# Splitting the node tiles into four chunks instead of three, and letting more expert steps into the rounds of a fused graph kernel

## The chip, the cores and the metric

The kernel runs on one core of one Trainium2 chip. The metric is device time in microseconds (us) of one execution. Engine names are those of the profile: PE is TensorE (PEld its weight loads), DVE is VectorE, ACT is ScalarE, POOL is GpSimd, SP is SyncE, which here only issues DMAs.

## The reference, cut to what matters

6,250 nodes of 256 features and 100,000 edges sorted by destination pass through four layers, each added to its input. All of it is float32.

```python
x = x + gat(layernorm(x), edges)              # attention, 8 heads: softmax over the edges of a node
x = x + moe32(layernorm(x))                   # top-1 of 32 experts: relu(relu(x W1[e] + b1) W2[e] + b2)
x = x + rgcn(layernorm(x), W[16], edges)      # out[dst] += norm * (x[src] @ W[rel])
x = x + moe8(layernorm(x), gamma, beta)       # 2 of 8 experts for the whole batch, then a layer norm
```

The change touches the second layer and the first half of the third: routing of each node to one of 32 experts, the two small matrix products of the expert, and the 16 products `x @ W[rel]` of each node, whose results are a table (`T_tab`) that the third layer gathers from edge by edge.

## The kernel before, in words

**Groups and rounds.** The edges are cut into 98 groups of 1,024. A first loop runs over `g` from 0 to 100; one pass is called a round here. For group `g`, POOL gathers 8 x 128 rows of `H_tab` by edge source (line L468, `hs`, five buffers); DVE scales them by the attention term (`gat_scale`, L603); PE sums them into a window of 128 nodes (`quarters`, L526, then `place`, L542); DVE adds the window into a ring of node tiles (`add`, L550). The parts of one group lie in successive rounds: round `g` adds group `g-3`, places group `g-2`, sums group `g-1` and gathers group `g`. So the two L550 additions of group `g-3` mark the start of round `g`, and round `r` lasts from the addition of group `r-3` to that of group `r-2`.

**Flow.** Beside the attention the same loop carries the next layer, in four kinds of step, each a Python generator (class `Flow`): kind 0, `take` (T), reads four finished node tiles out of the ring and normalizes them; kind 1, `route` (R), computes expert choices and slots, and at its end scatters all rows of the chunk into `x_sort`, sorted by expert (L902, POOL, one scatter per tile); kind 2, `experts` (E), walks over the sorted rows; kind 3, `products` (P), gathers the expert results back (L991, `yg`, POOL), normalizes and multiplies with the 16 relation matrices (L1037, two 512-column outputs per tile and relation pair, one P step each), writing `T_tab`.

**Chunks.** The 49 node tiles are cut into `CHUNKS`. A chunk's experts can begin only when its last row has been scattered, and its products only when its last expert step has been done. Every expert's rows are padded to a multiple of 128, so a chunk of `nt` tiles has up to `nt + 31` sorted tiles (`xt`). `experts` takes them in pairs: it loads 512 KB of sorted rows (L964, `xs`), two expert weight sets (L958, `w`, 192.5 KB each), transposes (L951), multiplies (L940, L928), adds on DVE (L930, `ys`, three buffers) and writes 256 KB (L974, `y_sort`). It is a pipeline of five further steps, so a chunk with `p` pairs takes `p + 5` E steps. All chunks share one `x_sort`; `route` of a chunk waits until the chunk before has read it (`ck.free`).

**Who decides the order.** The loop is recorded under a manual schedule for PE, DVE, ACT and SP: instructions stand on these engines in the order in which the Python code issues them. Once in every round, between the addition and the placement, `fill` draws steps. It has a budget of PE and of DVE microseconds, and each step returns its nominal cost (an E step 3.0 and 0.8, a P step 1.9 and 0.2). The kinds are tried in the order T, R, E, P, with a limit of each per round, as long as PE's budget lasts; all but P also need DVE's budget:

```python
if limits[kind] and left[0] > 0 and (kind == 3 or left[1] > 0):
```

When the 98 groups are over, the rest is drawn by `fill(2.5, 8.0, (1, 1, 1, 1))` until nothing is left. This is called the drain here. In it an E step spends the whole budget, so products wait until the experts of the last chunk are through. After the drain the third layer gathers from `T_tab` in a second loop of 98 groups (L468, `ts`), beside the fourth layer.

Of the kernel before, what the change touches and what calls it, by code (L numbers as in the profile page):

```python
# [47 lines left out]
def gnn_ffn_kernel(  # L48
# [31 lines left out]
    NT = (N + P - 1) // P  # L80
# [4 lines left out]

    RING = 8

    CHUNKS = [(0, 6), (6, 22), (22, NT)]


    blocks = [(t, min(4, NT - 1 - t), P) for t in range(0, NT - 1, 4)]
# [92 lines left out]

    largest = max(CHUNKS, key=lambda c: min(N, c[1] * P) - c[0] * P)
    chunks = [Chunk(*largest)]
    chunks = [chunks[0] if c == largest else Chunk(*c, x_sort=chunks[0].x_sort) for c in CHUNKS]
    whole = Chunk(0, NT)

    class Clear:  # L190
# [5 lines left out]
        def step(self, n):  # L196
            for c in range(self.done, min(self.done + n, self.n)):
                nc.sync.dma_start(self.rows[c], zeros[:, None, :].to_broadcast([P, 2 * D // P, P]))
            self.done = min(self.done + n, self.n)
# [352 lines left out]
    def gat_rows(gr):  # L552

        return gr.gather(H_tab[:, :], gr.idx0, HW, "hs", 1 if gr.dynamic else 5)

    def gat_dest(gr):

        oT = gr.onehot_t()
        if not gr.dynamic:
            return oT, gr.aw  # L560
        b = gr.block()
        aw = gr.pool.tile([P, 2 * HEADS], F32, name="aw")
        nc.vector.tensor_scalar(aw, adsh[:, ds(b, 1), :].rearrange("p o c -> p (o c)"), gr.win(0), None, op0=ALU.mult)
        nc.vector.scalar_tensor_tensor(aw, adsh[:, ds(b + 1, 1), :].rearrange("p o c -> p (o c)"), gr.win(1), aw,
                                       op0=ALU.mult, op1=ALU.add)
        return oT, aw

    def gat_pick(gr, parts, psum):

        oT, aw = parts  # L570
        pq = psum.tile([P, 512], F32, name="pe")
        ex = pq[:, T * 2 * HEADS : T * 3 * HEADS].rearrange("p (t h) -> p t h", t=T)
        if gr.dynamic:
            pe = pq[:, : T * 2 * HEADS].rearrange("p (t h) -> p t h", t=T)
            for t in range(T):
                nc.tensor.matmul(pe[:, t, :], lhsT=oT[:, t, :], rhs=aw, start=True, stop=True)
            return pe, ex

        w = Q * 2 * HEADS
        for u in range(QT):  # L580
            nc.tensor.matmul(pq[:, u * w : (u + 1) * w], lhsT=oT[:, u, :], rhs=aw.rearrange("p q h -> p (q h)"),  # L581
                             start=True, stop=True)
        return pq[:, : QT * w].rearrange("p (u q h) -> p q u h", u=QT, q=Q), ex

    def gat_terms(gr, hs, dest):

        pe, ex = dest

        z = gr.pool.tile([P, T, 2 * HEADS], F32, name="z")
        split = (lambda a: a) if gr.dynamic else (lambda a: a.rearrange("p (q u) h -> p q u h", u=QT))  # L590
        nc.vector.tensor_tensor(split(z), split(hs[:, :, D:]), pe, ALU.add)
        dz = gr.pool.tile([P, T, HEADS], F32, name="dz")
        nc.vector.tensor_tensor(dz, z[:, :, :HEADS], z[:, :, HEADS:], ALU.max)
        if gr.dynamic or gr.g == NG - 1:

            nc.vector.tensor_scalar_min(dz, dz, 0.0)
        nc.scalar.activation(ex, dz, AF.Exp)
        nc.scalar.copy(hs[:, :, D:HA], ex)  # L598

    def gat_scale(hs, dest):  # L600
        hv = hs[:, :, :D].rearrange("p t (h d) -> p t h d", h=HEADS)
        pv = dest[1].rearrange("p t (h o) -> p t h o", o=1)
        nc.vector.tensor_tensor(hv, hv, pv.to_broadcast([P, T, HEADS, HD]), ALU.mult)  # L603
# [484 lines left out]
    with ExitStack() as es_flow:  # L1088
        flow = Flow(es_flow, 2, 3)
        es = ExitStack()  # L1090
        pg = es.enter_context(tc.tile_pool(name="ge", bufs=2))
        pr1 = es.enter_context(tc.tile_pool(name="ge1", bufs=1))
        pp = es.enter_context(tc.tile_pool(name="ge_p", bufs=2, space=PSUM))
        pi = es.enter_context(tc.tile_pool(name="ge_i", bufs=1, space=PSUM))
        aws = [pr1.tile([P, Q, 2 * HEADS], F32, name=f"aw{i}") for i in range(6)]
        for a in aws:
            nc.vector.memset(a, 0.0)
        ring = Ring(pr1.tile([P, RING + 1, HA], F32, name="ring"))
        nc.vector.memset(ring.t, 0.0)

        done = [-1]

        def ready(tiles):

            return done[0] >= min(NG - 1, tiles * P * NG // N + 1)

        flow.after = lambda ck: tails.append(flow.products(ck))
        for before_ck, ck in zip([None] + chunks, chunks):
            ck.free = lambda c=before_ck: c is None or c.sorted
        takes = [flow.take(ck, ring, ready) for ck in chunks]  # L1110
        for ck in chunks:
            ck.taken = []
        routes = [flow.route(ck) for ck in chunks]
        runs, tails = [], []

        def step(kind):

            q = (takes, routes, runs, tails)[kind]
            while q:
                c = next(q[0], -1)  # L1120
                if c == -1:
                    q.pop(0)
                    if kind == 1:
                        runs.append(flow.experts(chunks[len(chunks) - len(q) - 1]))
                    continue
                return c
            return None

        left = [0.0, 0.0]

        def fill(pe, dve, limits):

            left[:] = min(left[0], 0) + pe, min(left[1], 0) + dve
            limits, any_ = list(limits), False
            while left[0] > 0:
                some = False
                for kind in range(4):
                    if limits[kind] and left[0] > 0 and (kind == 3 or left[1] > 0):
                        limits[kind] -= 1
                        c = step(kind)  # L1140
                        if c is None:
                            limits[kind] = 0
                            continue
                        some = any_ = True
                        left[:] = left[0] - c[0], left[1] - c[1]
                if not some:
                    break
            return any_


        with tc.manual_schedule(engines={PE, DVE, ACT, SP}):

            boot = flow.consts(cleared)
            groups = [Group(pg, g, False) for g in range(NG)]
            for g in range(4):
                if g < 3:
                    groups[g].load_dst()
                groups[g].load_terms(aws[g])
            dest = {0: gat_pick(groups[0], gat_dest(groups[0]), pp)}
            rows, hots, aggs, sums = {}, {}, {}, {}  # L1160
            for g in range(NG + 3):
                if g < NG:
                    rows[g] = gat_rows(groups[g])
                if g >= 3:
                    drained.append(ring.drained)
                    groups[g - 3].add(sums.pop(g - 3), HA, ring.t, True)
                    done[0] = g - 3
                if 2 <= g < NG + 2:
                    parts = groups[g - 2].leave(aggs.pop(g - 2), HA)
                if g < NG:  # L1170
                    hots[g] = groups[g].onehot(False)
                if g + 1 < NG:
                    oT = gat_dest(groups[g + 1])
                if g + 3 < NG:
                    groups[g + 3].load_dst()
                if g + 4 < NG:
                    groups[g + 4].load_terms(aws[(g + 4) % 6])
                next(boot, None)
                fill(6.5, 5.0, (3, 3, 3, 9))
                if 2 <= g < NG + 2:  # L1180
                    sums[g - 2] = groups[g - 2].place(pi, parts, HA)
                if g + 1 < NG:
                    dest[g + 1] = gat_pick(groups[g + 1], oT, pp)
                if 0 < g <= NG:
                    gat_scale(rows[g - 1], dest[g - 1])
                    aggs[g - 1] = groups[g - 1].quarters(pi, hots.pop(g - 1), rows.pop(g - 1), HA)
                if g < NG:
                    gat_terms(groups[g], rows[g], dest[g])
        es.close()
        with tc.manual_schedule(engines={PE, DVE, ACT, SP}):  # L1190
            while takes or routes or runs or tails:
                fill(2.5, 8.0, (1, 1, 1, 1))
# [598 lines left out]
```

## Time and profile before

| | us |
|---|---|
| median of 15 runs (3081.93 to 3092.66) | 3088.08 |
| the profiled execution's own time | 3084.9 |
| its span in the profile | 3083.1 |
| start to the first gather of the first loop | 112.4 |
| rounds 0 to 20, before the first expert step | 112.4 to 369.3 |
| rounds 21 to 99 | 369.3 to 1300.7 |
| round 100 and the drain, to the last product | 1300.7 to 1925 |
| second loop and fourth layer | 1925 to 3083.1 |

The times of rounds are read from the start of the L550 additions. Busy shares of the span are PE 73%, PEld 37%, DVE 38%, ACT 28% and POOL 54%, and the 16 DMA engines move 179 GB/s on average. These are averages over stages with different limits, so they are read stage by stage.

### The profile page before, as it was taken

The numbers are of one execution on the slowest core, as the hardware profiler recorded it, in microseconds if no ns is written. First come the engines' busy times: TensorE is split into PE (matmuls) and PEld (weight loads), VectorE is DVE, ScalarE is ACT, GpSimd is POOL, SyncE is SP. The second block draws the span as 40 slices with busy tenths as digits, with TensorE's granted clock in tenths as the row PEclk, the third lists the DMA queues.
The fourth block names the chain that finished last, engine by engine and source line by source line (L and its number), as shares of the span: only waits on it lengthen the run. The fifth ranks groups of instructions, "written<-read, shape, count | busy, mean of one in ns | idle before, by whom it ended". The sixth has DMA issues, their size and how long they took to land. (4 is left out here: it accounts for less than half of the span.)

```text
span 3083.1 us, 32452 instructions
## 1 busy us (share of the span) xinstructions
PE 2245.8 (73%) x8909; PEld 1153.3 (37%) x8910; DVE 1168.5 (38%) x3013; ACT 871.2 (28%) x1797; POOL 1661.6 (54%) x1712
## 2 busy tenths in 40 slices
PE   5534366688476688938999999566766666999984
PEld 4312144344344344416444444112322222555551
DVE  7444535557245555621100000123322222433457
ACT  2212223344233344413343343001111111222253
POOL 0477655777756777330000000777777777777724
PEclk9755566588666788978999999556766666999998
DMA  9567688577887577569544444633433333443424
GB/s 284 144 165 189 206 275 263 162 218 224 275 254 243 162 233 221 186 239 342 216 169 171 168 169 150 194 105 119 125 104 111 111 111 112 139 121 117 123 95 131
DMA packets 372122, 550.82 MB, mean 179 GB/s; under 512 B 88726, under 2 KB 234964, under 8 KB 371920
## 3 DMA queue, kind: packets, MB, share of 16 engines
q1 hardware_dynamic: 263964, 296.00, 28.5%
q0 software_dynamic: 82096, 231.26, 26.3%
q10 hardware_dynamic: 25860, 21.28, 2.3%
q8 instruction: 77, 1.26, 0.2%
q14 instruction: 125, 1.02, 0.1%
HBM read 355.59 MB, written 199.06 MB: 180 GB/s over the span
## 5 line engine op out<-in xcount | busy, mean ns | idle before, releaser
L468 POOL DMA_INDIRECT hs<-H_tab,src_i x784 | 760.9, 970 | 453.0 <-issue 210.5
L468 POOL DMA_INDIRECT ts<-T_tab,idx1b x784 | 755.8, 964 | 331.3 <-issue 233.1
L1037 PE MATMUL pb<-wr,xTt 128*128 128x512 f32 (+1 forms) x1568 | 710.1, 609 | 5.1 <-ACT xTt L1014 3.9
L526 PE MATMUL qagg<-ts,oh 128*32 128x256 f32 x1568 | 314.8, 509 | 192.5 <-DMA ts<-T_tab,idx1b 190.7
L1037 PEld LDWEIGHTS pb<-wr,xTt 128*128 128x128 f32 (+1 forms) x1568 | 299.7, 195 | 371.3 <-issue 356.4
L1040 ACT COPY tr<-pb 128x512 f32<-128x512 f32 (+1 forms) x392 | 228.3, 585 | 427.3 <-PE pb L1037 353.4
L533 ACT COPY qs<-qagg 128x264 f32<-128x264 f32 (+1 forms) x196 | 73.6, 376 | 881.6 <-PE qagg L526 858.5
L991 POOL DMA_INDIRECT yg<-y_sort,slot x49 | 47.1, 961 | 444.3 <-ACT xl L749 281.4
L581 PE MATMUL pe<-aw,oT 128*128 128x64 f32 x392 | 88.1, 368 | 265.9 <-DVE hs L603 90.5
L478 DVE TENSOR_TENSOR oh<-iota,rlm 128x256 f32<-128x256 f32 x196 | 83.3, 425 | 450.7 <-PE qagg L526 450.4
L526 PEld LDWEIGHTS qagg<-ts,oh 128*32 128x32 f32 x1568 | 66.1, 124 | 420.7 <-DMA ts<-T_tab,idx1b 352.6
L603 DVE TENSOR_TENSOR hs<-hs,pe 128x2048 f32<-128x2048 f32 x98 | 223.2, 2278 | 0.6 <-ACT hs L598 0.6
L542 PE MATMUL agg<-qs,pl 128*128 128x264 f32 (+1 forms) x392 | 177.4, 545 | 59.0 <-ACT qs L533 38.6
L1472 PE MATMUL pb<-xT,w 128*128 128x512 f32 (+2 forms) x416 | 196.0, 623 | 0.2 <-ACT xT L1442 0.2
L581 PEld LDWEIGHTS pe<-aw,oT 128*128 128x128 f32 x392 | 78.5, 273 | 311.3 <-issue 194.3
L1481 PE MATMUL pb<-w,h 128*128 128x256 f32 x784 | 175.4, 381 | 2.5 <-ACT h L1474 2.4
L346 DVE RECIPROCAL rst<-sdt 128x2 f32<-128x2 f32 (+1 forms) x25 | 4.1, 165 | 416.9 <-ACT sdt L344 416.9
L526 PE MATMUL qagg<-hs,oh 128*32 128x264 f32 x1568 | 159.3, 544 | 0.0
L1481 PEld LDWEIGHTS pb<-w,h 128*128 128x128 f32 x784 | 147.1, 190 | 28.7 <-issue 5.4
L550 DVE SCALAR_TENSOR_TENSOR ring<-agg,win,ring 128x264 f32 x196 | 96.6, 493 | 136.3 <-PE agg L542 102.9
L550 DVE SCALAR_TENSOR_TENSOR acc<-agg,win,acc 128x256 f32 x196 | 94.7, 483 | 136.3 <-PE agg L542 116.6
L542 PEld LDWEIGHTS agg<-qs,pl 128*128 128x128 f32 x392 | 86.5, 254 | 155.8 <-ACT qs L533 103.8
(297 smaller groups left out, 2461.0 us busy)
## 6 DMA issues: line engine op xcount, KB each, us to landing
T_tab<-tr SPq DMA_DIRECT2D x384, 256.0 KB
xs<-x_sort SPq DMA_DIRECT2D x70, 512.0 KB
w<-w_tab SPq DMA_DIRECT2D x142, 192.5 KB
y_sort<-ys SPq DMA_DIRECT2D x70, 256.0 KB
x_sort<-zeros SPq DMA_DIRECT2D x58, 256.0 KB
db<-in_dst_dram ACTq DMA_DIRECT2D x392, 32.0 KB
hs<-H_tab,src_i POOLq DMA_INDIRECT x784
ts<-T_tab,idx1b POOLq DMA_INDIRECT x784
```

The source lines that it names most:

```text
L468: nc.gpsimd.indirect_dma_start(out=hs[:, t, :], out_offset=None, in_=table, in_offset=bass.IndirectOffsetOnAxis(ap=idx(t), axis=0))
L478: nc.vector.tensor_tensor(oh, iota[:, None, :n].to_broadcast([P, T, n]), column(self.rl), ALU.is_equal)
L526: nc.tensor.matmul(ps[q * QW : (q + 1) * QW, :width], lhsT=oh[:, t, :], rhs=vals[:, t, :width], start=u == 0, stop=u == QT - 1)
L533: nc.scalar.copy(qs, ps[:, :width])
L542: nc.tensor.matmul(ps[:, :width], lhsT=pl, rhs=qs, start=True, stop=True)
L550: nc.vector.scalar_tensor_tensor(a, ps[:, :width], self.win(w), a, op0=ALU.mult, op1=ALU.add)
L581: nc.tensor.matmul(pq[:, u * w : (u + 1) * w], lhsT=oT[:, u, :], rhs=aw.rearrange("p q h -> p (q h)"), start=True, stop=True)
L603: nc.vector.tensor_tensor(hv, hv, pv.to_broadcast([P, T, HEADS, HD]), ALU.mult)
L1037: nc.tensor.matmul(pr[:r, :], lhsT=xT[:, k, j * P : j * P + r], rhs=self.wr[:, k, q0 : q0 + 2, :], start=k == 0, stop=k == KC - 1)
L1040: nc.scalar.copy(o2, pr[:r, :])
L1472: nc.tensor.matmul(ph[:, :nn], lhsT=s.w1[:, k, c * P : (c + 1) * P], rhs=xT[:, k, :nn], start=k == 0, stop=k == KC - 1)
L1481: nc.tensor.matmul(po[:, q * D : (q + 1) * D], lhsT=hid[c][:, (j + q) * P : (j + q + 1) * P], rhs=s.w2[:, c, :], start=c == 0, stop=c == N ...
```

## The change

`CHUNKS` gets four chunks, of 6, 12, 16 and 15 tiles, instead of 6, 16 and 27. In `fill`, E steps are no longer held back when DVE's budget is spent. In the rounds of the first loop, the limit of E steps goes from three to four, and PE's budget is 11.0 instead of 6.5 while no chunk is in its products (`tails` is empty).

```diff
-    CHUNKS = [(0, 6), (6, 22), (22, NT)]
+    CHUNKS = [(0, 6), (6, 18), (18, 34), (34, NT)]
...
-                    if limits[kind] and left[0] > 0 and (kind == 3 or left[1] > 0):
+                    if limits[kind] and left[0] > 0 and (kind > 1 or left[1] > 0):
...
-                fill(6.5, 5.0, (3, 3, 3, 9))
+
+                fill(6.5 if tails else 11.0, 5.0, (3, 3, 4, 9))
```

The numbers of pairs follow from the tile counts: 19, 24 and 29 in the three chunks before, 19, 22, 24 and 23 in the four after.

## The prediction

> **What bounds the kernel now.** I read the table of 40 slices first, then busy times by stretch. The stretches begin and end at L550 additions, so they are whole rounds: 21 to 34 (chunk 1's experts), 35 to 54, 55 and 56, 57 to 71 (chunk 2's experts), 72 to 99 (chunk 2's products); then the drain's routing, its scatters, chunk 3's experts, and products. The columns are length, busy time of PE, PEld, DVE, ACT and POOL, PE's granted clock, DMA share, GB/s.
>
> ```profile
> 369.30:556.90 187.60, 125.60 (x652) 81.72 (x651) 87.28 (x176) 55.87 (x142) 111.64 (x116) 0.65 0.80 249
> 556.90:768.00 211.10, 164.32 (x724) 83.81 (x727) 128.39 (x300) 92.07 (x195) 159.76 (x164) 0.81 0.70 206
> 768.00:811.60 43.60, 12.03 (x62) 7.75 (x63) 11.02 (x29) 4.56 (x13) 32.63 (x34) 0.50 0.78 264
> 811.60:1012.60 201.00, 143.53 (x761) 96.76 (x761) 102.01 (x201) 64.25 (x163) 120.31 (x123) 0.69 0.81 250
> 1012.60:1300.70 288.10, 237.97 (x1032) 119.49 (x1032) 157.29 (x336) 129.40 (x271) 197.14 (x203) 0.87 0.69 204
> 1300.70:1343.00 42.30, 29.44 (x94) 14.89 (x92) 25.97 (x106) 15.01 (x30) 0.02 (x1) 0.92 0.41 145
> 1343.00:1395.00 52.00, 7.17 (x15) 2.83 (x15) 0.27 (x2) 1.76 (x3) 26.53 (x27) 0.57 0.78 284
> 1395.00:1487.00 92.00, 81.90 (x467) 61.20 (x468) 20.04 (x30) 34.64 (x87) 0.00 (x0) 0.91 1.02 363
> 1487.00:1925.00 438.00, 435.22 (x1053) 194.32 (x1051) 21.63 (x124) 169.71 (x307) 26.20 (x27) 1.00 0.45 165
> ```
>
> Three regimes are to be seen. Rounds with products (rows 2 and 5) take 211.1/20 = 10.56 and 288.1/28 = 10.29 us, 10.4 together, a few idle ones included; POOL's gathers follow each other there at about 10 us per group. Rounds with experts take 201.0/15 = 13.4 us (row 4) at a DMA share of 0.81, with POOL busy only 60%: something other than gathers holds them. The drain's experts have the DMA engines saturated (1.02, 363 GB/s): 92 us for 29 pairs, 3.17 us a pair. The drain's products have PE saturated (435 of 438 us): 249 P steps, 1.76 us each.
>
> What holds an expert round is next, in the timeline of round 64, which draws three E steps.
>
> ```profile
> 909.88 1.02 DVE L550 SCALAR_TENSOR_TENSOR ring<-agg,win,ring 128x264 f32 x2 [0.34 <-PE agg L542]
> ...
> 925.66 0.69 DVE L930 SCALAR_TENSOR_TENSOR ys<-pb,xs 128x512 f32<-128x512 f32 x1 [9.51 <-DMA y_sort<-ys]
> ...
> 929.35 1.02 DVE L550 SCALAR_TENSOR_TENSOR ring<-agg,win,ring 128x264 f32 x2 [0.34 <-issue]
> ```
>
> From addition to addition it takes 19.5 us, and 9.51 of them DVE stands before `ys`, whose buffer is still being written to `y_sort`; everything behind it on DVE, `gat_scale` first, stands too. Expert rounds are bound by transfers, through an in-order engine. The last view is the waits from 768 to 825 us, where chunk 2's experts begin.
>
> ```profile
> PE pt L951 <- DMA xs<-x_sort: 25.2, 2, 23.8
> DVE ring L550 <- PE agg L542: 21.9, 1, 21.9
> ```
>
> PE waits for the first sorted rows, which wait for the last of 16 scatters, and the ring addition waits behind it. Rounds 55 and 56 took 43.6 us; at 13.4 each they would have taken 27, so a chunk of 16 tiles pays 17 us to begin.
>
> **The change part by part.** The instruction order of the built program, counted round by round, gives what moves. Rounds 0 to 20 draw the same T and R steps. Then:
> - before: 24 E steps in rounds 21 to 34, 29 in 55 to 71, products in the others, 34 E and 261 P in the drain;
> - after: 24 E in 21 to 27, products from 30 to 46, 27 E in 47 to 54, products from 58 on, 29 E mixed with one P a round in 80 to 100, 28 E and 255 P in the drain.
>
> So the smaller last chunk does not shorten the drain's products: only 6 P steps leave it, because chunk 3's 128 wait there instead. The loop gains 27 E steps: 21 new ones (16 pairs more by padding, 5 pipeline steps of one more chunk) and 6 from the drain.
>
> *The drain.* Its experts fall from 29 to 23 pairs, at 3.17 us: -19 us. Its scatters fall from 27 to 15, but the queue of POOL now has chunk 3's first six `yg` gathers ahead of and between them. 27 scatters took 41.5 us (1343.0 to 1384.5), 1.54 each; the new 21 POOL operations take between 21 x 1.28 = 27 and 32, and the third gather pair waits for a `yg` buffer, 0 to 8 more: -14 to -2, I take -10. Routing has 12 tiles fewer in its slot sums: four blocks instead of seven, each three DVE operations of 0.29 us, -2.6. After the last expert step there are 248 P steps instead of 249: -1.8. Sum: -33 us, bounds -37 and -25. The P steps of the routing part (12 before, 7 after) lie beside R steps; were that cover gone, 5 x 1.76 = 9 us would go as well.
>
> *Rounds 21 to 99 before: 931.4 us.* After, by kind of round:
> - 44 rounds with products or no steps (28 to 46, 55 to 79) at 10.4: 458 us. Density of T, R and P is as before.
> - 15 burst rounds (21 to 27, 47 to 54) with 3.4 E steps and 2.73 pairs each. Upper bound: the three-step round, 19.5, so 20. Lower bound by transfers: row 4 had 0.81 x 201 = 163 us of DMA time; its 22.5 pairs account for 71, leaving 6.1 per round; 6.1 + 2.73 x 3.17 = 14.8. By the chain of engines: an empty round takes 5.9 (two between 1012.6 and 1024.4), an E step 3.2 (from one L928 group to the next, 942.1 to 945.4), so 5.9 + 3.4 x 3.2 = 16.8. I take 18, nearer the three-step row: 270 us.
> - 20 mixed rounds (80 to 99) with 1.35 E and one P. Upper bound 13.4, as row 4 with 1.73 E. Lower bound 10.6, by transfers (6.1 + 1.2 x 3.17, and a P writes 0.26 MB) and by the gathers alike. E steps by row 4's price, (201 - 15 x 5.9)/26 = 4.33 with T and R in it, make 5.9 + 5.8 = 11.7; a P costs nothing if it fills a wait and 1.76 if not. I take 12.3: 246 us.
> - Waits for scatters: three chunks begin in this part instead of two. 17 us for chunk 3, somewhat less for 12 tiles, little for the first: 35, bounds 20 and 55.
>
> The sum is 1009, so +78 us; all lower bounds give 912, all upper bounds 1081.
>
> *The conditions in `fill`.* That E steps no longer need DVE's budget costs nothing itself: L930 is 0.69 us on a DVE that is busy 102 of 201 us. It is what makes the bursts. What stands behind each such L930 is `gat_scale`, and POOL waits for that through the five `hs` buffers. Eleven tiles fewer of `x_sort` to clear (256 KB each) free at most 11 x 0.256 MB / 250 GB/s = 11 us of transfers around rounds 19 to 30; I take that as part of the burst's range.
>
> *Second loop and fourth layer:* the same instructions in the same order, 1158 us, from a later start.
>
> Sum: +78 - 33 = +45 us on the profiled execution of 3084.9, so 3130. The median of the runs is 3.2 above that execution; on it the forecast is 3088 + 45 = **3133 us**.
>
> The loop's 22 additional pairs are 25.4 MB, 101 us at row 4's 250 GB/s and 70 at the 363 that experts reach without gathers; the bounds of the burst rounds lie as far apart. A rule that speaks against the change is in the Trainium skill, "DMA: Bandwidth & Descriptors", section "Issuing engines are not separate DMA queues": transfers started by any engine run on the same 16 DMA engines and interleave, so by it the gathers on POOL's queue give the experts on SP's queue no transfer time of their own. The page's "Where 436 GB/s comes from" puts the HBM limit of a core near 358 GB/s, by which, as an estimate, the 25.4 MB would take 71 us; the trace's 363 lies slightly above.
>
> In favour speaks row 4's clock, 0.69, against 0.91 where the drain's experts run back to back: denser bursts could run at the latter, where an E step takes 2.65 us (1413.00 to 1415.65): 15 x 3.4 x 0.55 = 28 us less, if the chain of engines held the bursts. By the 9.5 us before `ys` it doesn't, so I take nothing for it.
>
> **The rivals.** *A, bursts saturate the transfers, faster.* Mechanism: with four E steps in line DVE always has one whose buffer is free, so bursts run at the DMA floor of 14.8 us and mixed rounds at 10.6 to 11.5. Then the loop is 458 + 222 + 212 to 230 + 30 = 922 to 940, and the change -42 to -24: 3046 to 3064. For it: the drain does reach 1.02. Against: no round with gathers beside experts does; the three-step round shows a 9.5 us stall, not an overlap. It decides at 15 us per burst round with mixed rounds at 12.3, or 16.5 with mixed rounds at 11.2.
>
> *B, bursts starve the loop.* With `aw`, `xs`, `w` and `y_sort` on one SP queue, every wait for a buffer delays the next round's terms, so four-step rounds take 20 or more and each chunk pays its 17 us in full: +150 - 33 = +117, 3205. For it: `ACT pe L597 <- DMA aw<-ad_tab` is among the waits of row 4's stretch (15.3 us). Against: only the two E phases suffer.
>
> *C, the change does little.* Were the new E steps to fill POOL's idle 40% in expert rounds, loop and drain would balance: within 6 us of 3088. The drain's products being nearly as many is for it, the DMA share of 0.8 against.
>
> **How the numbers follow.** Forecast (+10 to +90 us): 0.60; A: 0.20; B (over +90): 0.13; C: 0.07. The range reaches into A and B until 0.15 is left out, 3052 to 3198; the forecast's own is 3098 to 3178. Faster by over 0.2% (about what a measurement of this kernel can tell from no change): 0.20; within: 0.07; slower: 0.73.
>
> **What would show it.** In the profile after, round 28 should begin near 500 us (before 472), round 47 near 698 (694), round 55 near 857 (768), round 80 near 1117 (1102), round 100 near 1378 (1301). The drain from there to the last product should take 592 us, not 624. Burst rounds should show L930 waiting for `y_sort` at a DMA share near 0.9. A is right if burst rounds come at 15 us. The forecast is wrong if round 100 begins before 1344.

## The result

The changed kernel takes 3125.21 us (median of 6 runs, 3118.6 to 3126.34; the profiled run and one more took 3124.94 and 3130.65) against 3087.24 for the kernel before (31 runs): a ratio of 1.0119, with an interval of 1.0108 to 1.0131. It is slower by 38 us; the forecast was slower by 45. The profiled execution has a span of 3123.2 us, against 3083.1.

The first view is again the busy time by stretch, cut at L550 additions, with the columns explained above: rounds 21 to 27, 28 to 46, 47 to 54, 55 to 78, 79 alone, 80 to 99; then the drain's routing, its scatters, chunk 4's experts and the products. Kernel after:

```profile
371.70:501.40 129.70, 95.79 (x470) 65.50 (x469) 46.10 (x89) 38.32 (x98) 60.28 (x64) 0.67 0.81 265
501.40:704.60 203.20, 159.63 (x706) 81.95 (x709) 124.27 (x294) 93.36 (x194) 148.89 (x152) 0.81 0.70 205
704.60:868.40 163.80, 105.19 (x532) 72.32 (x524) 58.24 (x110) 43.22 (x110) 77.49 (x81) 0.68 0.79 260
868.40:1130.00 261.60, 211.97 (x914) 108.45 (x914) 151.73 (x358) 118.04 (x247) 196.95 (x204) 0.84 0.73 219
1130.00:1161.20 31.20, 6.79 (x39) 3.76 (x37) 5.52 (x15) 6.68 (x15) 22.79 (x24) 0.67 0.82 276
1161.20:1377.20 216.00, 172.79 (x957) 107.30 (x957) 121.32 (x243) 81.77 (x203) 121.69 (x126) 0.83 0.84 263
1377.20:1418.00 40.80, 25.54 (x74) 12.86 (x72) 23.26 (x92) 10.48 (x21) 3.77 (x4) 0.78 0.37 129
1418.00:1460.00 42.00, 2.90 (x11) 1.89 (x11) 1.53 (x7) 1.97 (x4) 17.03 (x17) 0.50 0.67 235
1460.00:1530.00 70.00, 63.75 (x365) 47.59 (x363) 16.30 (x25) 27.45 (x69) 0.00 (x0) 0.92 1.00 358
1530.00:1970.00 440.00, 433.02 (x1050) 193.38 (x1050) 21.78 (x125) 169.84 (x307) 24.31 (x25) 1.00 0.46 165
```

Read it by the same regimes. Rounds with products (rows 2 and 4) run as before, 10.69 and 10.90 us each. Bursts (rows 1 and 3) run at 18 us a round, round 47's wait aside, with PE at two thirds of its clock and the DMA engines at 0.8, no fuller than the expert rounds of before. The mixed rounds (row 6) take 10.8 us each, and at a share of 0.84 they are the fullest rounds with gathers in either kernel. The drain's experts last 70 us between these cuts, and 73.5 from their first transpose (1456.1), which is where the 92 of before begin; the share is saturated in both. The products take 440 instead of 438.

| stage (us) | before | after | change |
|---|---|---|---|
| up to round 21 | 369.3 | 371.7 | +2.4 |
| rounds 21 to 99 | 931.4 | 1005.5 | +74.1 |
| round 100 to the first `ts` gather | 632.2 | 596.7 | -35.5 |
| from there to the end of the span | 1150.2 | 1149.3 | -0.9 |

How a burst runs is seen in the timeline of round 49, which draws four E steps. It is the counterpart of round 64 above; the brackets give the idle time before, and what ended it.

```profile
763.63 1.02 DVE L550 SCALAR_TENSOR_TENSOR ring<-agg,win,ring 128x264 f32 x2 [0.48 <-PE agg L542]
...
779.25 0.69 DVE L930 SCALAR_TENSOR_TENSOR ys<-pb,xs 128x512 f32<-128x512 f32 x1 [8.44 <-DMA y_sort<-ys]
...
783.35 0.69 DVE L930 SCALAR_TENSOR_TENSOR ys<-pb,xs 128x512 f32<-128x512 f32 x1 [3.40 <-DMA w<-w_tab]
...
787.02 1.02 DVE L550 SCALAR_TENSOR_TENSOR ring<-agg,win,ring 128x264 f32 x2 [0.33 <-PE pe L581]
```

It lasts 23.4 us, and for 8.44 of them DVE stands before the third `ys`, whose buffer is still being written out, as it did for 9.51 before. Before the fourth, the profile puts 3.40 us down to the weights, a transfer again.

Each chunk still pays to begin. Two waits of round 47, where chunk 2's experts start:

```profile
PE pt L951 <- DMA xs<-x_sort: 31.6, 1, 31.6
DVE ring L550 <- PE agg L542: 29.7, 1, 29.7
```

PE stands before the first sorted rows and the ring addition behind it. Round 47 lasts 39.7 us where the other seven of its burst average 17.7, so the start costs 22. Chunk 3's start falls into round 79, 31.2 us against 10.9 for the rounds before it, so 20.

### The profile page after: what moved, and what is told of

It is laid out like the page before. It is cut to its first block, busy times and chain, and to the rows that moved or that the text cites. A ratio compares the mean times of both kernels' runs of the same rounds, so it can differ in the third digit from the quotient of the medians.

```text
span 3123.2 us, 33300 instructions
## 1 busy us (share of the span) xinstructions
PE 2283.8 (73%) x9163; PEld 1185.1 (38%) x9164; DVE 1183.8 (38%) x3068; ACT 894.9 (29%) x1851; POOL 1660.8 (53%) x1712
## 5 line engine op out<-in xcount | busy, mean ns | idle before, releaser
L1037 PE MATMUL pb<-wr,xTt 128*128 128x512 f32 (+1 forms) x1568 | 725.3, 618 | 6.1 <-ACT xTt L1014 6.0
L542 PE MATMUL agg<-qs,pl 128*128 128x264 f32 (+1 forms) x392 | 168.7, 521 | 55.9 <-ACT qs L533 36.5
L930 DVE SCALAR_TENSOR_TENSOR ys<-pb,xs 128x512 f32<-128x512 f32 (+1 forms) x88 | 60.0, 682 | 267.7 <-PE pb L928 127.8
L951 PE MATMUL pt<-ident,xs 128*128 128x128 f32 x346 | 70.8, 338 | 110.4 <-DMA xs<-x_sort 109.6
L526 PE MATMUL qagg<-hs,oh 128*32 128x264 f32 x1568 | 149.6, 515 | 1.6 <-DVE hs L603 1.1
L550 DVE SCALAR_TENSOR_TENSOR ring<-agg,win,ring 128x264 f32 x196 | 96.6, 493 | 134.9 <-PE agg L542 103.5
```

The costliest lines, as they stand in the source:

```text
L526: nc.tensor.matmul(ps[q * QW : (q + 1) * QW, :width], lhsT=oh[:, t, :], rhs=vals[:, t, :width], start=u == 0, stop=u == QT - 1)
L542: nc.tensor.matmul(ps[:, :width], lhsT=pl, rhs=qs, start=True, stop=True)
L550: nc.vector.scalar_tensor_tensor(a, ps[:, :width], self.win(w), a, op0=ALU.mult, op1=ALU.add)
L1037: nc.tensor.matmul(pr[:r, :], lhsT=xT[:, k, j * P : j * P + r], rhs=self.wr[:, k, q0 : q0 + 2, :], start=k == 0, stop=k == KC - 1)
```

## The experiments

The later runs, e1 to e11, were made on three other chips (e1 to e4 on one, e5 to e8 on the next, e9 to e11 on the third), where the kernel before takes 3490 to 3520 us. Ratios below are against it on the same chip, and stages are compared within a chip except where the text says otherwise. Why these chips are slower is a question of its own (last section).

**The two halves apart.** One run has only the new chunks, the other only the new rules of `fill`.

```diff
 # e1: the kernel before with
-    CHUNKS = [(0, 6), (6, 22), (22, NT)]
+    CHUNKS = [(0, 6), (6, 18), (18, 34), (34, NT)]
 # e2: the kernel after with
-    CHUNKS = [(0, 6), (6, 18), (18, 34), (34, NT)]
+    CHUNKS = [(0, 6), (6, 22), (22, NT)]
```

> The four chunks with the old fill (PE budget 6.5, at most three E steps, E steps need DVE's budget). Counted in the instruction order: rounds 21 to 34 as before, chunk 2's and chunk 3's E steps mixed with about one P a round (rounds 46 to 67 and 79 to 99), 32 E and 289 P steps in the drain, 285 of the P steps after the last expert step (before 249, changed kernel 248). Theory 'starts and padding' (the two edits cost separately and add): rounds 21 to 99 take 188 + 33 rounds of products at 10.7 + 42 mixed rounds at 10.8 + two starts of 20 = 935 us against 931 before; the drain gains 33 us as in the changed kernel and loses 36 x 1.76 = 63, so about +30 us on before, 3117. Rival 'the bursts are the whole loss, a fourth chunk is free': within 10 us of before, 3088 to 3098. Rival 'the fourth chunk alone costs all': 3125 or more.

> Three chunks as before with the new fill. Counted in the order: E steps in bursts, rounds 21 to 27 and 55 to 62, 28 P steps more in the loop and 28 fewer after the drain's experts. Theory (edits add): rounds 21 to 99 take 130 + 170 for the bursts as the changed kernel showed and 64 x 10.7 = 685 for the others, 985 against 931, +54; the drain -28 x 1.76 = -49: together +5 us, 3092. Rival 'bursts are the whole loss': 35 to 40 us slower than before, 3125. Rival 'bursts free rounds for products': the burst rounds cost nothing over the spread ones and the 28 products come for nothing, 40 us faster than before, 3045.

Measured: the chunks alone (e1) 3513.89 us, ratio 1.0070 (1.0046 to 1.0095); `fill` alone (e2) 3490.5, ratio 0.9984 (0.9964 to 1.0004). The product is 1.0054, and the whole change, run again later (e6), gave 1.0050 (1.0024 to 1.0075). So the chunks carry the loss. The rules of `fill` are not told from no change here, and whether they give some of the loss back can't be told either, as the intervals of 1.0070 and 1.0050 overlap.

The stages show why. For before, the loop is taken from e3 (below), which has the same instructions in rounds 21 to 99 and ran on the same chip, and the drain from e5, on another of these chips. A P step is one 512-column output, eight for each tile.

| us | before | chunks only | `fill` only |
|---|---|---|---|
| start of round 21 | 426.5 (e3) | 435.2 | 427.4 |
| rounds 21 to 99 | 1105.5 (e3) | 1086.5 | 1148.7 |
| round 100 to first `ts` | 633.3 (e5) | 663.0 | 590.7 |
| P steps after the last E step | 249 | 285 | 221 |

With the old budget the new chunks' E steps push products out of the loop: round 100 begins 10 us earlier (1521.7 against 1532.0) although the loop holds 23 more E steps, and 36 P steps, 63 us at 1.76, reappear in the drain, of which the smaller last chunk saves only about 33. That makes +19, near the +21 of the medians. Of the 19 us by which rounds 21 to 99 are shorter, 9 stand before round 21 instead, because the first chunk's scatters come a round earlier (last section). The expectation had +4 for these rounds and +30 for the drain. With the old chunks the new rules move 28 P steps into the loop: +43 us there, -43 in the drain, as near to nothing as expected (+5). The whole change does both, and ends with the products of the drain where they were (248), so the drain keeps its 33 and the loop bears the E steps. What looked like one trade, experts out of the drain for a longer loop, is two trades of which one cancels.

**The two kernels again.** Both were run unchanged on one later chip, as a reference for the others.

> The kernel before, once more, for its stages on the chip of the runs beside it. The runs before this one fell on a chip on which the kernel before takes 3492 us, so stages are compared with a run of the same chip. All theories: where the chip is as in the first profiles, round 100 starts at 1301 and the span is 3083; on the other, 3490.

> The changed kernel once more, beside the kernel before on the same chip. Theory: 1.2% slower where the kernel before takes 3087 us. Where it takes 3492 us, waits for transfers are longer in all rounds, so the additional expert pairs weigh less against the same bases: 0 to 1.2% slower. By adding the two edits as measured there (chunks alone 1.0070, fill alone 0.9984): 1.0054.

Measured: before (e5) 3512.9 us in one run, against a median of 3520.14 on that chip; after (e6) 3535.72, ratio 1.0050. Rounds 21 to 99 took 1114.3 and 1163.7, +49 where the first chip had +74; the drain 633.3 and 597.6, -35.7 where it had -35.5. So the drain's saving is the same to a microsecond on both chips, and the smaller ratio comes from the loop. Counted to the start of round 100, the profiles differ by 59.5 us, where the first chip had 76.5. Gather-fed rounds are longer there: product rounds take 13.3 us (rounds 28 to 46) instead of 10.7. That longer rounds cover more of the added E steps would fit, but it was not tried by itself.

**What holds a burst: transfers or engines.** Half of the weight loads are left out, and each pair's second tile uses the first one's weights; the arithmetic instructions stay.

```diff
                     for j in range(lv["n"]):
-                        w = pool.tile([P, B1C + 1], F32, name="w", bufs=8)
-                        nc.sync.dma_start(w, w_tab[ds(lv["e"][j], 1)].rearrange("o p w -> (o p) w"))
+                        if j == 0:
+                            w = pool.tile([P, B1C + 1], F32, name="w", bufs=8)
+                            nc.sync.dma_start(w, w_tab[ds(lv["e"][j], 1)].rearrange("o p w -> (o p) w"))
                         lv["w"].append(w)
```

> The changed kernel with one weight load per pair instead of two (the second tile of a pair uses the first one's weights): 192.5 KB of 1153 KB of a pair's transfers left out, all instructions of PE, ACT and DVE kept. Theory 'burst rounds are bound by transfers': 17% less per pair, 2.73 x 0.53 = 1.4 us less per burst round, so 10 us less in rounds 21 to 27 and 11 in 47 to 54, and 12 less in the drain's experts: some 35 us less in all. Rival 'burst rounds are bound by the chain of PE, ACT and DVE (16.8 us)': burst stretches unchanged within 4 us each, only the drain's 12 us less. Mixed rounds (80 to 99) unchanged at 10.8 by both, if the gathers hold them.

Measured: busy time by stretch of rounds 21 to 27, 47 to 54, 80 to 99 and of the drain's experts, first for the changed kernel whole (e6):

```profile
440.30:573.60 133.30, 90.18 (x471) 63.07 (x470) 46.00 (x89) 38.01 (x98) 53.94 (x57) 0.72 0.78 245
825.50:995.20 169.70, 110.13 (x531) 75.69 (x528) 58.32 (x109) 42.88 (x110) 71.58 (x73) 0.65 0.76 246
1353.60:1604.00 250.40, 188.52 (x958) 115.08 (x958) 120.83 (x243) 81.13 (x203) 123.83 (x127) 0.76 0.75 230
1682.40:1755.00 72.60, 66.50 (x372) 49.73 (x372) 15.87 (x24) 27.60 (x70) 0.00 (x0) 0.90 1.01 363
```

The same stretches with half the weight loads (e4), the last one again from the first transpose to the last addition, and two steps out of it:

```profile
437.50:561.40 123.90, 90.21 (x469) 63.01 (x469) 46.01 (x89) 37.74 (x98) 53.96 (x57) 0.72 0.73 235
810.30:967.00 156.70, 105.24 (x532) 72.77 (x532) 58.07 (x109) 42.84 (x110) 71.67 (x73) 0.69 0.74 240
1326.20:1563.70 237.50, 181.60 (x959) 111.88 (x959) 120.22 (x243) 80.35 (x203) 124.10 (x126) 0.81 0.73 222
1641.40:1708.80 67.40, 65.32 (x372) 48.22 (x372) 15.86 (x24) 27.37 (x70) 0.00 (x0) 0.92 0.93 324
...
1676.34 0.69 DVE L930 SCALAR_TENSOR_TENSOR ys<-pb,xs 128x512 f32<-128x512 f32 x1 [1.96 <-PE pb L928]
...
1678.98 0.69 DVE L930 SCALAR_TENSOR_TENSOR ys<-pb,xs 128x512 f32<-128x512 f32 x1 [1.96 <-PE pb L928]
```

The counts on DVE and ACT are nearly the same in each pair of rows. The bursts become 9.4 and 13.0 us shorter, the mixed rounds 12.9 and the drain's experts 5.2, about 40 in all. PE's busy time falls by 0.0, 4.9, 6.9 and 1.2 of these, and in the last three its clock is higher; the rest is time without work. The product rounds 28 to 46, without weight loads, take 248.9 us in e4 and 251.9 in e6. So transfers bind the bursts, and not the chain of engines: 0.5 to 0.6 us less for each pair, where 0.53 was expected. The edit also takes work off SP, whose instructions last 72.4 us in the first of these stretches in e6 and 53.9 in e4. SP is not full with that, but how much of the gain is bytes and how much SP's queue, the run doesn't tell apart. That the mixed rounds gain just as much was not expected: those were taken to be held by the gathers. The drain's experts gave 5 us instead of 12. With half the weights their steps follow each other 2.64 us apart at a DMA share of 0.93, with PE busy for 65.3 of 67.4 us: there the chain of engines takes over, at the 2.65 us a step that the prediction read from the trace before.

The two profiles come from two chips on which the kernel before takes about the same time. In e11, on the third, the same bursts and mixed rounds of whole weight loads take 132.5, 167.6 and 249.1 us, within 2.1 of e6. With other values a later part of the program went another way and the span became 3914 us; only the stages up to the drain are read.

**What a chunk pays to begin.** In the trace after, ACT waits in round 79 for a write of the product table:

```profile
ACT tr L1040 <- DMA T_tab<-tr: 22.7, 1, 22.7
```

This write stands on SP's queue behind the loads of rows to be scattered. One theory says that the hold of SP makes the start expensive, the other that the start waits for the scatters themselves. The run takes these loads from SP's queue.

```diff
-                node_dma(nc.sync, xs2[:, None, :], x1_tab, a + j, 1, r, False)
+                node_dma(nc.gpsimd, xs2[:, None, :], x1_tab, a + j, 1, r, False)
```

> The changed kernel with the row loads of route (L114, xs2 from x1_tab) issued by POOL instead of SP; everything else as it is. Theory 'at a chunk's start SP is held by row loads that wait for buffers freed by scatters, and T_tab writes and the terms of the next rounds stand behind them': round 79, 31 us after the change, falls to 15 or less, and round 47 (40 us), where PE waits for the first sorted rows, falls by under 10. POOL gets one more DMA of some 1 us per tile, 43 in the loop, so 10 to 25 us less in all. Rival 'the start waits for the scatters themselves': rounds 47 and 79 keep their lengths within 5 us, and POOL's additional DMAs make the whole 0 to 40 us slower.

Measured (e7): 3536.89 us in one run, beside 3535.72. Round 47 takes 30.6 us instead of 34.3. Rounds 79 and 80 become shorter, 16.4 and 9.2 instead of 20.5 and 16.5, but round 81 takes 26.8 instead of 12.0, and rounds 79 to 82 together 64.8 instead of 61.5. So a wait is met two rounds later, and freeing SP's queue gains nothing in all. That the start is paid for the scatters fits, but is not shown, as the trace names nothing that ends the longest wait of round 81 (21.9 us).

**A version that beats both.** In the drain of before, the 27 scatters and the wait behind them leave PE nearly idle, while 249 products wait until after the experts. If `route` hands back control after each scatter of the last chunk, a product can be drawn after each.

```diff
-                if j % 8 == 7:
+                if j % 8 == 7 or ck.b == NT:
                     yield 0, 0.1
```

> The kernel before; only route of the last chunk yields after every scatter instead of after every eighth, so that in the drain one P step stands behind each of the 27 scatters. Theory 'what is idle in the drain is PE, waiting for the scatters, with products ready': 24 P steps move from behind the experts to the 52 us of the scatters, 24 x 1.76 = 42 us less, 3046; L1037 begins to fill the stretch from 1343 to 1395. Rival 'SP's queue is held by the row loads that wait for buffers freed by scatters, so T_tab writes behind them cannot leave, and with three tr buffers the products stand still': under 10 us less, 3078 to 3088.

> The kernel before with the yield after every scatter of the last chunk, once more, as the base of the run beside it. Theory 'products fill the scatters' time in the drain': 0.990 to 0.993 of the kernel before where that takes 3490 to 3520 us (30 us), 0.990 where it takes 3087: the P steps after the experts 24 fewer, 42 us, and the stretch of scatters 10 us longer, because T_tab writes and scatters share the transfers. Rival 'the first ratio was chance': within 0.3% of the kernel before.

Measured: 3462.57 us (e3), ratio 0.9906 (0.9872 to 0.9939), and on the third chip (e9) 3482.78, ratio 0.9919 (0.9886 to 0.9952). Scatters, experts and products of the drain, busy time by stretch, in the kernel before (e5):

```profile
1588.20:1642.00 53.80, 6.80 (x12) 2.64 (x12) 0.11 (x1) 1.76 (x3) 26.61 (x27) 0.56 0.78 277
1642.00:1732.00 90.00, 79.44 (x466) 59.63 (x467) 20.03 (x30) 34.70 (x87) 0.00 (x0) 0.94 1.03 372
1732.00:2177.80 445.80, 435.50 (x1053) 194.27 (x1051) 22.44 (x128) 170.65 (x308) 26.27 (x27) 0.99 0.45 165
```

The same three with the edit (e9):

```profile
1582.40:1648.30 65.90, 50.94 (x114) 20.47 (x112) 1.54 (x7) 17.47 (x31) 26.47 (x27) 0.90 0.87 322
1648.30:1744.60 96.30, 86.20 (x467) 64.04 (x468) 20.05 (x29) 34.72 (x87) 0.00 (x0) 0.88 0.98 348
1744.60:2147.00 402.40, 392.15 (x953) 175.05 (x951) 21.19 (x121) 154.55 (x280) 26.20 (x27) 1.00 0.46 167
```

PE's busy time among the scatters goes from 7 to 51 us, and the products behind the experts lose 43. The scatter stretch itself grows by 12; that the products' table writes share its transfers (0.87 instead of 0.78) fits. So about 30 of the expected 42 remain. The rows shown give 25, because e9's experts take 96 us; in e3 they take 91, and its drain, 604.7 us from round 100 to the first `ts` gather, is 28.6 shorter than e5's.

The same edit was put on the two kernels with the new `fill`:

> Three chunks, the new fill, and the yield after every scatter of the last chunk. Theory 'products can fill the scatters' time in the drain': fill alone was even with the kernel before; here 16 of chunk 2's last products stand among the scatters, so 16 x 1.76 = 28 us less than the kernel before, less than the 30 us that the yield alone brought to it (24 products). Rival 'the burst edit and the spread need the same time': no faster than the kernel before within 6 us.

> The changed kernel with the yield after every scatter of the last chunk: 14 P steps move from behind the last experts to among the 15 scatters. Theory 'products fill the scatters' time': 14 x 1.76 = 25 us less behind the experts, the stretch of scatters up to 10 us longer, so 15 to 25 us less than the changed kernel: 1.000 to 1.007 of the kernel before where that takes 3087, 0.998 to 1.001 where it takes 3500. Rival 'the row loads on SP hold the T_tab writes': no less than the changed kernel.

Measured: on `fill` alone (e8) 3522.78 us, ratio 1.0005 (0.9979 to 1.0032). The expectation had miscounted: where the loop has taken the products in already, only 5 more move among the scatters (221 to 216). On the whole change (e11) 3508.59, ratio 1.0001 (0.9961 to 1.0041): with 14 moved, the drain falls from 597.6 to 584.8 us, 13 of the 18 us that the change lost on these chips. The interval still overlaps that of the change without it.

The last run sits on e3 and spreads the products within the loop: a larger budget where chunk 2's experts and products run, and at most two P steps a round up to round 71.

```diff
-                fill(6.5, 5.0, (3, 3, 3, 9))
+                fill(6.5 if g < 54 or g > 78 else 7.5, 5.0, (3, 3, 3, 2 if g < 72 else 9))
```

> The kernel beside it, with at most two P steps a round until round 71 and a PE budget of 7.5 in rounds 54 to 78: chunk 1's products last until chunk 2's experts, so that rounds 55 to 66 draw 1.5 E steps and one P each, as the mixed rounds of the changed kernel, instead of 1.7 E steps alone; chunk 2's products begin in round 76 instead of 75, and 226 P steps follow the last expert step (225 beside it). Theory 'expert rounds are bound by transfers': the same pairs and P writes pass in rounds 55 to 75 either way, so within 8 us of the kernel beside it. Rival 'mixed rounds are cheap because P steps fill the waits of the experts' chain': the rounds with experts fall from 13.4 to 10.8 as in the changed kernel (on the slower chips from 14.8 to 12.5), 30 us or more less than the kernel beside it.

Measured (e10): 3476.11 us, ratio 0.9914 (0.9888 to 0.9940), 7 us from e9 and not to be told from it. Rounds 55 to 75 and 76 to 99, first in e9:

```profile
914.30:1247.20 332.90, 195.93 (x934) 128.19 (x930) 132.02 (x269) 84.20 (x208) 185.22 (x191) 0.61 0.66 206
1247.20:1538.00 290.80, 222.77 (x921) 110.72 (x916) 137.61 (x296) 112.09 (x238) 159.19 (x162) 0.87 0.58 174
```

and in e10:

```profile
919.60:1234.40 314.80, 194.19 (x965) 120.00 (x965) 130.62 (x261) 86.29 (x213) 177.78 (x183) 0.70 0.69 214
1234.40:1541.00 306.60, 238.91 (x940) 117.33 (x940) 139.31 (x302) 119.47 (x247) 163.24 (x166) 0.83 0.56 171
```

The first stretch is 18 us shorter, the second 16 longer. Of the 18, 13 lie in rounds 55 to 57, as 11 of the chunk's 16 scatters come before round 55 here, and rounds 47 to 54 are 8 longer for it. This is what the theory of transfers expected (within 8 us); the 30 us of the rival did not come. Products beside experts don't by themselves make the rounds cheap.

## Why the prediction was right

The sum was +45 us and the result +38, for the reason given: only six E steps leave the drain, and 21 new ones come with the fourth chunk. The round starts were close up to the second burst and at the end: round 28 at 501.4 (forecast 500), round 47 at 704.6 (698), round 55 at 868.4 (857), round 100 at 1377.2 (1378). Between them they were not: round 80 began at 1161.2 instead of 1117. Of these 44 us, 11 were there at round 55, 12 come from dearer product rounds, and 21 are chunk 3's start, which fell into round 79 while the forecast counted it after round 80 began. The mixed rounds were then 30 us cheaper than taken. By terms:

| term (us) | forecast | measured |
|---|---|---|
| rounds with products, and a plain round 79 (44) | 458 | 203.2 + 261.6 + 10.9 = 475.7 |
| burst rounds (15) | 270 | 129.7 + 163.8 - 22 = 271.5 |
| mixed rounds (20) | 246 | 216.0 |
| starts of chunks 2 and 3 (chunk 1's is in its burst) | 35 | 22 + 20 = 42 |
| sum, rounds 21 to 99 | 1009 | 1005.5 |
| drain's experts | -19 | 92.0 to 73.5: -18.5 |
| drain's scatters | -10 | 41.5 to 27.3: -14.2 |
| drain as a whole | -33 | -35.5 |
| up to round 21, second loop and fourth layer | 0 | +1.5 |

- *Bursts.* The size was right, and the reason in kind: transfers, through `ys` and DVE, as e4 shows. The 18 us themselves were picked between floors of 14.8 and 16.8 and a ceiling of 20, so part of the hit is luck. The bursts move 265 and 260 GB/s, hardly more than the 249 and 250 of the expert rounds before. That they gain no transfer time from having experts on SP's queue and gathers on POOL's agrees with the rule weighed in the prediction (the Trainium skill, "DMA: Bandwidth & Descriptors", section "Issuing engines are not separate DMA queues"). Sharing alone doesn't say why the share stops at 0.8. A DMA share near 0.9 was a miss; it stayed at 0.81 and 0.79. The clock in bursts did not rise either (0.67 and 0.68), so the 28 us were rightly left out. A pair's 1,153 KB are of 1,024 bytes, so the 22 pairs are 26.0 MB and 104 us, not 25.4 and 101; nothing rests on it.
- *Mixed rounds* are the term that was mis-sized. 12.3 was taken by the price of an E step in an expert round; measured were 10.8. That this is next to the lower bound of 10.6 is chance: the DMA engines were busy for 0.84 x 10.8 = 9.1 us a round and POOL for 56% of the time, so neither was full. By bytes the price would have come closer. A mixed round moves 2.84 MB (263 GB/s over 216.0 us, 20 rounds), a round of row 4 in the prediction 3.35 MB, and 2.84 MB at row 4's 250 GB/s take 11.4 us. So, as an estimate, 0.9 of the 1.5 us too much come from counting steps instead of bytes, and 0.6 from a rate 5% higher. e4 shows that these rounds too wait for transfers, and e10 that products beside the experts are not enough to make them cheap. This saved 30 us, and dearer product rounds (10.69 and 10.90 for 10.4) and dearer starts took back 25. The total is closer than its terms, and that the two cancel is luck.
- *Scatters.* The price was between the bounds and at the better one: of the six `yg` gathers that POOL draws, four came before the first scatter, and only two stood among them. From round 100 to the last product the drain took 589 us (forecast 592).
- *Rival A* (bursts at the floor of the transfers, 14.8 us) was wrong at 18, though its mixed rounds came true. *Rival B* asked for +150 in the loop, which had +74. Its price of a start, 17 us in full, was exceeded, 22 and 20. *Rival C* was wrong by 38 us, but its ground holds: the drain's products stayed.

Rounds 0 to 20 draw the same steps, as predicted, but the first chunk's six scatters run in round 20 after and in round 21 before; on the first chip this cost nothing (256.8 and 256.9 us for these rounds).

Not foreseen was that the two parts of the diff work against each other in the drain. The prediction took the order of the built program with both, and so summed the right steps; the two halves were needed to see that the chunks alone would have put 36 P steps into the drain.

## What to carry to other kernels

Cutting work finer moves it out of an exposed tail but also adds padding and pipeline steps; count both from the built order, here 6 steps moved and 21 added, before a price is put on either. Where transfers hold a round, its bytes price it better than its steps: rounds with experts, alone, in bursts or beside products, all moved 249 to 265 GB/s on the first chip, while the time for each step differed. And look for idle PE beside the exposed wait before rearranging the loop: a hand-back after each scatter, one line, brought 0.8 to 0.9% in two runs where the whole change lost 0.5 to 1.2%.

## What the runs showed that was not expected

The same program takes 3087 us on the first chip and 3490 to 3520 on three others, and the difference lies where POOL's gathers feed the loop. The second loop on the first chip, kernel before, in the view by stretch:

```profile
1932.90:2927.20 994.30, 741.79 (x2949) 330.89 (x2952) 320.43 (x793) 153.68 (x265) 755.75 (x784) 0.73 0.41 122
```

The same loop of the same kernel in e5:

```profile
2177.80:3335.10 1157.30, 597.79 (x2857) 313.15 (x2858) 311.72 (x765) 143.63 (x251) 758.91 (x784) 0.69 0.36 105
```

POOL spends the same time on the same 784 gathers (755.75 and 758.91 us), and the drain, which has few, takes 632 and 633 us, but this loop takes 163 us more and rounds 0 to 20 take 317 instead of 257. In e5's waits over the whole span the largest is one that the profile puts down to no instruction of this core:

```profile
ACT qs L533 <- remote: 880.0, 82, 38.2
```

Much of that is only the label: records of matmuls are missing (2857 are in the loop's row above, 2949 on the first chip), and on the first chip the same line's waits, 858.5 us, are put down to PE's sums (`qagg`). But all its waits together grow from 881.6 to 1315.5 us, about as much as the span (428 us). The gathers themselves don't show it: the packets of POOL's queue, 48 for each gather of this loop, end a median 2.41 us after its issue on the first chip and 2.43 in e5. What does is PE: by its records it stands idle for more than 5 us 31 times in this loop of e5, 404 us together, and never on the first chip. Why it stands the trace does not say, and it stays open.

On the later chips rounds 0 to 20 took some 7 us longer with four chunks than with three. All of it is round 20, 18 us long in e1 and e6 and 10 in e3 and e5. With four chunks it holds the first chunk's six scatters (423.9 to 430.3 us in e6), which with three fall into round 21 (434.0 to 440.3 in e5).

The drain's experts, with all their weights and no gathers beside them, move 354 to 372 GB/s at a DMA share of 1.00 to 1.03 on the first chip and the next two, and 334 to 348 at 0.96 to 0.98 on the third. None of the stretches of rounds shown, with gathers, came above 276 GB/s and 0.84. Why transfers hold DVE at a share of 0.8 was not tried apart. The Trainium skill, "DMA: Bandwidth & Descriptors", section "Where 436 GB/s comes from", gives about 358 GB/s as the HBM limit of a core; 363 and 372 GB/s over 92 and 90 us were measured, loads and stores together, so here that figure was not a ceiling.
